# Keys and values of each token tile in a buffer of their own, in a ring of eight

## The chip, the cores and the metric

The kernel runs on one core of one Trainium2 chip. The metric is the device time of one execution in microseconds; the median over several executions counts. Before the change three executions took 2259.31, 2259.92 and 2261.94 us, with a median of 2259.92 us.

## What is computed

The reference is one transformer block over 32 sequences of 512 tokens with 256 features, all in float32. The first half is attention over a window of 128 tokens with 16 query heads and 4 key and value heads of width 64; the second half is a linear layer with eight gated low-rank corrections.

```python
x = x + attn(layernorm(x))      # q = x @ wq.T, k = x @ wk.T, v = x @ wv.T
                                # q, k = rmsnorm(q), rmsnorm(k), per head
                                # mask = (i >= j) & (i - j < 128)
                                # softmax(q @ k.T / 8, masked) @ v, then @ wo.T
x = x + ffn(layernorm(x))       # xt @ weight.T + 1/16 * sum over the experts of
                                # softmax(xt @ gate_w.T) * (xt @ U.T) @ V.T
```

## The kernel before

The 32 sequences are cut into 128 token tiles of 128 tokens, four to a sequence. The host lays the weights out, and the core keeps them in SBUF for the whole run. Because the window is as long as a tile, a token tile needs only its own keys and values and those of the tile before it in the same sequence.

The work is a software pipeline whose order is written out by hand. The function `slot(i)` lists, for one step, which part of which tile comes next, and the program calls it for i from 0 to 134. The order of that list is the order of the instructions in the queue of every engine: TensorE (PE), VectorE (DVE), ScalarE (ACT), GpSimd (POOL) and SyncE (SP). No scheduler moves anything. A tile is spread over eight slots: in slot i the projections of tile i are made, in slots i + 2 and i + 3 its scores and exponentials, in slot i + 4 the probabilities are transposed and moved by DMA, in slot i + 6 they are multiplied by the values, and in slot i + 7 the second half ends and the result is stored. Waits between engines are semaphore waits that the language puts in: one wherever an instruction touches a buffer, or a bank of PSUM, that another engine uses, unless an earlier wait in the same queue has already covered it.

Keys and values of a tile come out of one product, `kv_pe` (L289), into a PSUM bank named `kv_ps`, with 256 columns of keys and 256 of values. Four steps use that bank:

- `ksq` (L300), on ScalarE, squares the keys for their norm.
- `vdiff` (L471 and L474), on VectorE, forms `vd`, the difference between the tile's own values and those of the tile before it. It reads the own values from `kv_ps` and the old ones from the SBUF buffer `kv`. It does nothing for the first tile of a sequence, so it runs for 96 of the 128 tiles.
- `kv_copy` (L296), on ScalarE, scales keys and values and writes them to the SBUF buffer `kv`.

In `slot` these stand in the order `ksq(i)`, `vdiff(i)`, `kn(i - 1)`, `kv_copy(i)`, `qn(i - 1)`, `kT_copy(i - 2)`.

The SBUF buffer `kv` is read in three places: by `kn` (L337, GpSimd), which normalises the keys in slot i + 1; by `vdiff` of the next tile, also in slot i + 1; and by `y_pe` (L485, TensorE), where it is the stationary operand of the products with the probabilities. `y_pe` of a tile reads the values of that tile and of the one before, so the values of tile i are read for the last time in slot i + 7.

Before the change, one buffer holds keys and values of a whole sequence. It is taken when the first tile of the sequence is written, and there are three of them:

```python
if self.t == 0:
    self.s.kv = seq.tile([P, NT, 2 * KD], F32, tag="kv", name=f"kv_{self.b}", bufs=3)
nc.scalar.activation(self.s.kv[:, self.t, :], self.ps["kv"], AF.Copy, scale=self.ln1.rs)
```

Of the kernel before, what the change touches and what calls it, by code (L numbers as in the profile page):

```python
# [8 lines left out]
F32 = mybir.dt.float32  # L9
I32 = mybir.dt.int32  # L10
AF = mybir.ActivationFunctionType
# [3 lines left out]
P = 128  # L15
D = 256
HD = 64
# [13 lines left out]
def tile_window_attn_lora_ffn(  # L31
# [42 lines left out]
    nc = tc.nc  # L74
    B, T, _ = x.shape
    NT = T // P
# [4 lines left out]
    KD = KV * HD  # L81
# [14 lines left out]
    seq = ctx.enter_context(tc.tile_pool(name="seq", bufs=3))  # L96
# [16 lines left out]
    def bank(what, name):  # L113
# [19 lines left out]
        "other": 3,  # L133
        "tr": 2,
        "pT": 2,
    }

    def buf(what, shape, name):
        return work.tile(shape, F32, tag=what, name=f"{what}_{name}", bufs=BUFS[what])
# [109 lines left out]
    class Tile:  # L249
# [41 lines left out]
                )  # L291

        def kv_copy(self):
            if self.t == 0:
                self.s.kv = seq.tile([P, NT, 2 * KD], F32, tag="kv", name=f"kv_{self.b}", bufs=3)
            nc.scalar.activation(self.s.kv[:, self.t, :], self.ps["kv"], AF.Copy, scale=self.ln1.rs)  # L296

        def ksq(self):
            self.k_sq = buf("ksq", [P, KD], self.n)
# [35 lines left out]
        def kn(self):  # L335
            self.k_n = buf("kn", [P, KD], self.n)
            nc.gpsimd.tensor_tensor(  # L337
                self.k_n.rearrange("p (g d) -> p g d", d=HD),
                self.s.kv[:, self.t, :KD].rearrange("p (g d) -> p g d", d=HD),
                self.rs[:, NH:].unsqueeze(2).to_broadcast([P, KV, HD]),  # L340
                ALU.mult,
            )
# [121 lines left out]
        def vdiff(self):  # L464

            if self.t == 0:
                return
            self.vd = buf("vd", [P, KD], self.n)
            own, old = self.ps["kv"][:, KD:], self.s.kv[:, self.t - 1, KD:]
            lo, hi = slice(0, H), slice(H, P)  # L470
            nc.vector.scalar_tensor_tensor(  # L471
                self.vd[lo], own[lo], self.ln1.rs[lo], old[lo], ALU.mult, ALU.subtract
            )
            nc.vector.scalar_tensor_tensor(  # L474
                self.vd[hi], own[hi], self.minus_rs[hi], old[hi], ALU.mult, ALU.add
            )

        def y_pe(self):


            ps = [self.bank(f"y{e}") for e in range(2)]

            def product(gp, half, e, v, w, start, stop):
                v0 = (2 * gp + half) * HD
                nc.tensor.matmul(  # L485
                    ps[e][half * HD : (half + 1) * HD, gp * 4 * H : (gp + 1) * 4 * H],
                    v[:, v0 : v0 + HD],
                    w.rearrange("p h (c a q) -> p a h c q", c=2, a=2)[:, half],
                    start=start, stop=stop, skip_group_check=True,
                )  # L490

            for gp in range(GP):
                for e in range(2):
                    v = self.s.kv[:, max(self.t - 1 + e, 0), KD:]
                    for half in range(2):
                        product(gp, half, e, v, self.probs(gp, e), gp == 0, self.t == 0)
            if self.t > 0:
                for gp in range(GP):
                    for half, e in ((0, 0), (1, 1), (1, 0), (0, 1)):
                        rows = slice(e * H, (e + 1) * H)  # L500
                        product(gp, half, e, self.vd[rows], self.other[gp][rows], False, True)
# [92 lines left out]
    tiles = {}  # L594
# [132 lines left out]
```

## Time and profile before

| what | value |
|---|---|
| median of three executions | 2259.92 us |
| the profiled execution: its own time | 2258.15 us |
| the profiled execution: its span, first to last instruction | 2256.2 us |
| mean granted TensorE clock | 0.989 |
| busy: PE, POOL, DVE, ACT | 2145.9, 1807.1, 1734.7, 1508.3 us |
| `kv_copy` L296: 128 instructions, mean | 686 ns |
| `vd` L471 and L474: 96 instructions each, mean | 473 and 491 ns |
| `kn` L337: 128 instructions, mean | 612 ns |
| products `y_ps<-pT,kv` L485: 2048 instructions, busy | 250.1 us |

The span is the time between the first and the last instruction on the core; the execution's own time has 1.95 us more around it. A product in float32 appears in the trace as more than one matrix instruction, so the counts on TensorE are larger than those in the source. A wait in the trace names the engine that sat idle and the instruction whose end released it; idle time of an engine that is not on the chain that ended last costs nothing by itself.

### The profile page before, as it was taken

What the parts mean: (1) busy time and instruction counts of PE and PEld (TensorE: products, weight loads), DVE (VectorE), ACT (ScalarE), POOL (GpSimd) and SP (SyncE); (2) the same over time, 40 slices, a digit from 0 to 9 for tenths busy, and PEclk for the clock granted to TensorE, in tenths of its full rate; (3) what the DMA queues carried; (4) which work ended last, traced back from release to release, by engine and by line L of the source; (5) the groups of instructions that cost most, each with busy time, mean ns of one, the idle gap of its engine ahead of it and who ended that gap; (6) DMA issues with size and microseconds to landing.
All of it is one profiled execution on the core that took longest, in us unless ns stands there. A gap on an engine that the chain in (4) does not pass through costs nothing.

```text
span 2256.2 us, 43995 instructions
## 1 busy us (share of the span) xinstructions
PE 2145.9 (95%) x12688; PEld 1340.5 (59%) x12688; DVE 1734.7 (77%) x4300; ACT 1508.3 (67%) x5889; POOL 1807.1 (80%) x1771
## 2 busy tenths in 40 slices
PE   5799999999999999999999999999999999999997
PEld 2366566666566666566666566666566666566654
DVE  3577877777877777877777877777877777877773
ACT  2567667767767767767767767767767767767762
POOL 3598788888888888888888888888888888888873
PEclk8799999999999999999999999999999999999999
DMA  2344444544544454544544544544544544544542
GB/s 93 72 111 116 119 118 114 120 118 114 120 118 114 118 120 114 123 116 114 122 117 113 123 116 114 123 116 113 123 116 114 123 116 113 123 116 114 123 112 65
DMA packets 140127, 257.77 MB, mean 114 GB/s; under 512 B 37872, under 2 KB 73840, under 8 KB 139888
## 3 DMA queue, kind: packets, MB, share of 16 engines
q1 hardware_dynamic: 137472, 251.81, 46.5%
q10 hardware_dynamic: 2416, 3.16, 0.4%
q8 instruction: 103, 1.69, 0.3%
q14 instruction: 136, 1.11, 0.2%
HBM read 19.93 MB, written 16.78 MB: 16 GB/s over the span
## 4 chain that ended last, share of the span: by engine, by line
PE 66%; ACT 17%; DVE 9%; issue 4%; SPq 2%; DMA 1%; POOL 1%; ACTq 1%; DVEq 0%; POOLq 0%
PE y_ps L485 14%; PE s_ps L387 13%; PE q_ps L305 12%; ACT ex L414 12%; PE kv_ps L289 8%; PE f_ps L543 7%; PE o_ps L512 5%; PE f_ps L581 2%; ACT kT L369 2%; DVE nmax L403 2%; PE hT_ps L530 2%; DVE vd L474 2%; DVE vd L471 2%; SPq L244 2%; PE xT_ps L277 1%
## 5 line engine op out<-in xcount | busy, mean ns | idle before, releaser
L414 ACT ACTIVATE ex<-s_ps,nmax 128x128 f32<-128x128 f32 x2048 | 722.1, 381 | 13.2 <-DVE nmax L403 11.7
L426 POOL TENSOR_TENSOR ex<-ex,rden 128x1024 f32<-128x1024 f32 x256 | 479.9, 1896 | 130.9 <-DVE rden L422 125.8
L305 PE MATMUL q_ps<-wq_sb,xT 128*128 128x512 f32 x1024 | 489.0, 600 | 3.2 <-ACT qsq L318 3.2
L512 PE MATMUL o_ps<-wo_sb,yT 128*128 128x256 f32 x2048 | 463.5, 379 | 3.7 <-ACT yT L506 3.7
L214 POOL TENSOR_TENSOR rs<-rs,minus_half 128x20 f32<-128x20 f32 x128 | 457.5, 3574 | 10.7
L512 PEld LDWEIGHTS o_ps<-wo_sb,yT 128*128 128x128 f32 x2048 | 388.6, 190 | 110.2 <-issue 58.4
L414 ACT ACTIVATION_READ_ACCUMULATOR ex<-s_ps,nmax 128x1 f32 x2048 | 454.0, 222 | 0.0
L387 PEld LDWEIGHTS s_ps<-kT,pT 64*128 64x128 f32 x4000 | 276.5, 187 | 194.6 <-ACT ex L414 135.6
L387 PE MATMUL s_ps<-kT,pT 64*128 64x160 f32 (+4 forms) x4000 | 329.7, 300 | 45.9 <-ACT ex L414 45.9
L403 DVE TENSOR_REDUCE nmax<-s_ps 128x4 f32<-128x512 f32 x512 | 353.8, 691 | 17.6
L457 POOL TENSOR_SCALAR_AFFINE_SELECT other<-pT 64x512 f32<-64x512 f32 x384 | 299.9, 781 | 22.2 <-DMA pT<-tr 9.5
L305 PEld LDWEIGHTS q_ps<-wq_sb,xT 128*128 128x128 f32 x1024 | 187.2, 193 | 150.1 <-issue 129.4
L437 DVE STREAM_TRANSPOSE tr<-ex 128x256 f32<-128x256 f32 (+3 forms) x512 | 239.7, 487 | 29.1 <-DMA pT<-tr 25.0
L289 PE MATMUL kv_ps<-wkv_sb,xT 128*128 128x512 f32 x512 | 257.8, 626 | 1.0 <-ACT xT L283 1.0
L485 PE MATMUL y_ps<-pT,kv 128*64 128x256 f32 x2048 | 250.1, 386 | 0.5 <-ACT xT L283 0.5
L506 ACT COPY yT<-y_ps 128x512 f32<-128x512 f32 x256 | 138.6, 599 | 160.6 <-PE y_ps L485 160.6
L346 POOL TENSOR_TENSOR qn<-q,rs 128x1024 f32<-128x1024 f32 x128 | 243.4, 1901 | 0.0
L398 DVE COPY_PREDICATED s_ps<-over,s_ps 128x128 f32<-128x128 int32 x512 | 149.5, 292 | 98.9 <-PE s_ps L387 94.4
L300 ACT ACTIVATE ksq<-kv_ps,ln_rs_a 128x256 f32<-128x256 f32 x128 | 60.6, 473 | 243.3 <-PE kv_ps L289 232.3
L485 PEld LDWEIGHTS y_ps<-pT,kv 128*64 128x64 f32 x2048 | 136.1, 137 | 128.0 <-ACT q L313 50.8
L543 PE MATMUL f_ps<-wf_sb,hT 128*128 128x392 f32 x512 | 193.2, 500 | 18.0 <-ACT xT L283 12.1
L313 ACT ACTIVATE q<-q_ps,ln_rs_a 128x512 f32<-128x512 f32 x256 | 182.7, 714 | 27.9 <-PE q_ps L305 27.9
(83 smaller groups left out, 2716.3 us busy)
## 6 DMA issues: line engine op xcount, KB each, us to landing
pT<-tr SPq DMA_DIRECT2D x2000, 104.0 KB, 2.2
x<-in_x_dram SPq DMA_DIRECT2D x128, 128.0 KB, 2.3
out_dram<-res SPq DMA_DIRECT2D x128, 128.0 KB, 1.9
pT<-tr SPq DMA_DIRECT2D x48, 64.0 KB, 2.0
wq_sb<-in_wq_dram ACTq DMA_DIRECT2D x1, 1024.0 KB, 7.1
wo_sb<-in_wo_dram ACTq DMA_DIRECT2D x1, 1024.0 KB, 9.3
pT_-3_205<-tr_-3_199 SPq DMA_DIRECT2D x16, 40.0 KB, 1.9
pT_-2_274<-tr_-2_268 SPq DMA_DIRECT2D x16, 40.0 KB, 1.9
```

The costliest lines, as they stand in the source:

```text
L214: nc.gpsimd.tensor_tensor(o, o, minus_half[:, :n], ALU.pow)
L289: nc.tensor.matmul(ps, self.xT[:, c, :], wkv_sb[:, c, :], start=(c == 0), stop=(c == ND - 1))
L305: nc.tensor.matmul(ps, self.xT[:, c, :], wq_sb[:, c, gp * 512 : (gp + 1) * 512], start=(c == 0), stop=(c == ND - 1),)
L346: nc.gpsimd.tensor_tensor(self.q_n.rearrange("p (g d) -> p g d", d=HD), self.q.rearrange("p g (h d) -> p (g h) d", d=HD), self.rs[:, :NH]. ...
L387: nc.tensor.matmul(ps[:, half, gp, o0:n], qT[rows, gp * P : (gp + 1) * P], self.s.kT[rows, gp, k0 + o0 : k0 + n], start=True, stop=True,)
L403: nc.vector.tensor_reduce(self.nmax[j], ps[:, :, :, :P], AX.X, ALU.max, negate=True)
L414: nc.scalar.activation(self.ex[e][:, c, gp, half], ps[:, gp, half, :P], AF.Exp, bias=self.nmax[j][:, gp, half : half + 1], accum_out=self. ...
L426: nc.gpsimd.tensor_tensor(ex, ex, self.rden[e].rearrange("p c g a -> p (c g a)").unsqueeze(2).to_broadcast([P, 8, P]), ALU.mult,)
L457: nc.gpsimd.affine_select(out=self.other[gp][rows].rearrange("p h (c a q) -> p h c a q", c=2, a=2), in_=fr.rearrange("p h (c a q) -> p h c ...
L485: nc.tensor.matmul(ps[e][half * HD : (half + 1) * HD, gp * 4 * H : (gp + 1) * 4 * H], v[:, v0 : v0 + HD], w.rearrange("p h (c a q) -> p a ...
L512: nc.tensor.matmul(ps[:, :D], self.yT[:, c].rearrange("p e t -> p (e t)"), wo_sb[:, c, :], start=(c == 0), stop=(c == NCH - 1),)
L543: nc.tensor.matmul(ps[:, : UG + D], self.hT[:, c, :], wf_sb[:, c, :], start=(c == 0), stop=(c == ND - 1),)
```

## The change

Each tile gets a buffer of its own for its keys and values, 128 partitions by 512 floats, and eight of these buffers are used in turn. The first tile of a sequence no longer takes a larger buffer. The readers name the buffer of the tile they want in place of a slice of the sequence's buffer. In a partition the ring takes 8 x 2 KiB = 16 KiB, where three sequence buffers of 8 KiB took 24 KiB. No line of `slot` is changed.

```diff
@@ the table of buffer counts
         "pT": 2,
+        "kv": 8,
@@ kv_copy
-            if self.t == 0:
-                self.s.kv = seq.tile([P, NT, 2 * KD], F32, tag="kv", name=f"kv_{self.b}", bufs=3)
-            nc.scalar.activation(self.s.kv[:, self.t, :], self.ps["kv"], AF.Copy, scale=self.ln1.rs)
+            self.kv = buf("kv", [P, 2 * KD], self.n)
+            nc.scalar.activation(self.kv, self.ps["kv"], AF.Copy, scale=self.ln1.rs)
@@ kn
-                self.s.kv[:, self.t, :KD].rearrange("p (g d) -> p g d", d=HD),
+                self.kv[:, :KD].rearrange("p (g d) -> p g d", d=HD),
@@ vdiff
-            own, old = self.ps["kv"][:, KD:], self.s.kv[:, self.t - 1, KD:]
+            own, old = self.ps["kv"][:, KD:], tiles[self.i - 1].kv[:, KD:]
@@ y_pe
-                    v = self.s.kv[:, max(self.t - 1 + e, 0), KD:]
+                    v = tiles[self.i - 1 + e if self.t > 0 else self.i].kv[:, KD:]
```

## The prediction

> **What bounds the kernel now.** I read the page's first part, then the chain that ended last, then the waits, and then every row in which the buffer `kv` is written or read. The first part and the chain:
>
> ```profile
> span 2256.2 us, 43995 instructions
> ...
> PE 2145.9 (95%) x12688; PEld 1340.5 (59%) x12688; DVE 1734.7 (77%) x4300; ACT 1508.3 (67%) x5889; POOL 1807.1 (80%) x1771
> ...
> PE 66%; ACT 17%; DVE 9%; issue 4%; SPq 2%; DMA 1%; POOL 1%; ACTq 1%; DVEq 0%; POOLq 0%
> PE y_ps L485 14%; PE s_ps L387 13%; PE q_ps L305 12%; ACT ex L414 12%; PE kv_ps L289 8%; PE f_ps L543 7%; PE o_ps L512 5%; PE f_ps L581 2%; ACT kT L369 2%; DVE nmax L403 2%; PE hT_ps L530 2%; DVE vd L474 2%; DVE vd L471 2%; SPq L244 2%; PE xT_ps L277 1%
> ```
>
> TensorE is busy 95% of the span and carries 66% of the chain. The rest goes mostly over ScalarE (17%) and VectorE (9%). The two instructions of `vdiff` are themselves on the chain with 2% each: so what stands around `kv_copy` matters, and a change of its waits could be seen. The waits that concern this step, from the list of who waited for whom (total us, times, longest us):
>
> ```profile
> ACT ksq L300 <- PE kv_ps L289: 232.3, 125, 5.9
> ACT kv L296 <- DVE vd L474: 115.7, 96, 1.7
> PE s_ps L387 <- ACT ex L414: 61.0, 101, 3.8
> DVE vd L471 <- ACT ksq L300: 31.8, 65, 3.3
> ```
>
> ScalarE sits idle 115.7 us in all, 1.2 us in each of 96 tiles, in front of `kv_copy`, until `vdiff` is done. That is the only wait in front of any writer or reader of `kv` that is worth a name, and the only one that the change could seem to lift. In time order, over one and a half slots (start us, length us):
>
> ```profile
> 975.80 0.61 PE L485 MATMUL y_ps<-other,vd 64*64 64x256 f32 x8
> ...
> 979.71 0.47 ACT L300 ACTIVATE ksq<-kv_ps,ln_rs_a 128x256 f32<-128x256 f32 x1 [1.89 <-PE kv_ps L289]
> 980.22 0.48 DVE L471 SCALAR_TENSOR_TENSOR vd<-kv_ps,ln_rs_a,kv 64x256 f32<-64x256 f32 x1 [0.54 <-ACT ksq L300]
> 980.71 0.49 DVE L474 SCALAR_TENSOR_TENSOR vd<-kv_ps,minus_rs,kv 64x256 f32<-64x256 f32 x1
> 981.24 0.69 ACT L296 ACTIVATE kv<-kv_ps,ln_rs_a 128x512 f32<-128x512 f32 x1 [1.05 <-DVE vd L474]
> ...
> 997.35 0.69 ACT L296 ACTIVATE kv<-kv_ps,ln_rs_a 128x512 f32<-128x512 f32 x1 [1.05 <-DVE vd L474]
> ```
>
> `ksq`, the two halves of `vd` and `kv_copy` follow one another and never overlap. All four read the PSUM bank `kv_ps`. `vd` waits for `ksq`, with which it shares no SBUF buffer that `ksq` writes, so what orders those two can only be the bank. By the same reasoning `kv_copy` waits for `vd` because of the bank: it writes slice t of `kv`, and `vd` reads slice t - 1.
>
> **What the Trainium skill says.** "PSUM — Partial Sum Buffer", section "PSUM bank collisions raise a hardware error", states that two engines must not be on the same bank and quadrant at once, reads against reads included, and that software must guard it with semaphores. The trace agrees: 96 waits of `kv_copy` for the 96 tiles that have a `vd`, and none for the 32 first tiles. "SBUF — State Buffer", section "Who interferes with whom", states that only the port pair shared by VectorE and GpSimd causes contention; nothing in it depends on the address within a partition. The trace agrees as far as it can, since `kv` before lies at 12 places (three buffers of four slices) and its rows have hardly any spread (min/median/max ns):
>
> ```profile
> L485 PEld LDWEIGHTS y_ps<-pT,kv x2048: 132/137/232, 110.5 to 2239.8; 128*64 128x64 f32 x187
> L296 ACT ACTIVATE kv<-kv_ps,ln_rs_a x128: 679/687/692, 18.3 to 2165.9; 128x512 f32<-128x512 f32 x128
> L337 POOL TENSOR_TENSOR kn<-kv,rs x128: 612/612/615, 30.0 to 2180.4; 128x256 f32<-128x256 f32 x128
> L471 DVE SCALAR_TENSOR_TENSOR vd<-kv_ps,ln_rs_a,kv x96: 465/476/477, 26.1 to 2164.9; 64x256 f32<-64x256 f32 x96
> L474 DVE SCALAR_TENSOR_TENSOR vd<-kv_ps,minus_rs,kv x96: 490/491/494, 26.6 to 2165.4; 64x256 f32<-64x256 f32 x96
> ```
>
> "DMA: Bandwidth & Descriptors", section "How a descriptor splits into AXI transactions", states that a transfer's start is counted in steps of 256 bytes. That matters because buffers move (below); no run here shows a misaligned transfer.
>
> **The change part by part.**
>
> *Instructions.* The four edits name other addresses and add or remove nothing. In the two programs as built, every engine has the same instructions in the same order: cost 0.
>
> *The wait of `kv_copy` for `vd`.* It would go only if it came from the SBUF buffer. It comes from the bank, and in the changed program as built it is still there, for the same 96 copies: gain 0.
>
> *The wait for a free buffer.* Before, a buffer was reused 12 tiles later and asked for only at the first tile of a sequence; now every copy overwrites the buffer of the tile eight before. The last reader of tile i - 8 is `y_pe` of tile i - 7, in slot i - 1. The extract shows it: the last products of one slot start at 975.80 us and are over at 976.41, those that read `kv` even earlier, and the copy of the next slot starts at 997.35, 20.9 us later, more than one slot (981.24 to 997.35 is 16.1 us). The other readers, `kn` and `vd`, are done in slot i - 7. ScalarE has by then passed its own wait for the same products, in `y_copy` of slot i - 1, and waits on VectorE and GpSimd newer than the other readers. So nothing has to be waited for, and no waiting instruction has to be added; every semaphore wait in the two programs as built has the same semaphore and the same value. Cost 0. The cover is 20.9 us thick; it would shrink by one slot with seven buffers, and with six the reader would stand behind the writer.
>
> *Addresses.* This is all that is left. The ring frees 8 KiB in a partition, so all buffers laid out behind it move: `x`, `xT`, `kT` and `ksq` down by 24 KiB, `q`, `tr`, `pT`, `ex` and the rest by 8 KiB, `kv` itself up by 23 KiB. These are multiples of 256 bytes, so no transfer changes its alignment: the DMAs (`x` 2.3 us, `pT` 2.2 us from issue to landing) should stay as they are. For the instructions on `kv` I bound the effect from both sides by the spread of their own rows: `kv_copy` 13 ns x 128 = 1.7 us, `vd` (12 + 4) ns x 96 = 1.5 us, `kn` 3 ns x 128 = 0.4 us, together 3.6 us, were all of it on the path. The weight loads from `kv` take 137 ns beside products of 379, and are hidden even if they doubled. The DMA waits that are worth a name (VectorE 25.0, GpSimd 9.5, ScalarE 2.4 us for `pT`) are 36.9 us; an estimate of 5% either way for them gives 1.8 us. So between -5.4 and +5.4 us; I take 0, since no row shows a dependence on the place.
>
> *Sum.* Against the profiled execution: span 2256.2 + 0, with 1.95 us around it 2258.15 us. The median of the runs stands 1.77 us above that execution, so the forecast is 2259.9 us, no change.
>
> **The rivals.**
>
> *Faster: the wait for `vd` goes after all.* For it: 115.7 us of idle ScalarE, and `vd` on the chain. Then `kv_copy`, `kT_copy` and the exponentials behind it would run up to 1.2 us earlier in 96 tiles. What TensorE gains is bounded by what it loses to late exponentials, 61.0 us: 2259.9 - 61 = 2199 us; the outer bound is 2259.9 - 115.7 = 2144. Against it: the bank orders the two, and it still does. Chance 3%.
>
> *Slower: a new wait in front of each copy.* With eight buffers each copy, not each fourth, has to be sure of three readers on three engines. Were that one more waiting instruction on ScalarE's queue, it would stand in front of `kT_copy` and the exponentials that TensorE waits for. The chain in order of time shows what such an entry of ScalarE's sequencer costs (start us, length us):
>
> ```profile
> 1015.07 0.02 ACT kv L296
> 1015.09 0.04 issue
> 1015.13 0.04 ACTq L369
> 1015.17 0.04 issue
> ```
>
> That is 0.04 and 0.04 us, 0.08 x 128 = 10 us, so 2270 us, if the entry stands behind the wait for `vd`; ahead of it, the 1.2 us of idle would hide it. It decides from 35 ns per tile (4.5 us over 128). Against it: the waits as built are the same. Chance 3%.
>
> *The places matter.* Some row or transfer is longer or shorter at its new place by more than the spread above. Twice the bound is 11 us: 2249 or 2271. For it: nothing but that it is the only thing that differs. Chance 6%, half of it on each side.
>
> **How the numbers follow.** About 0.2%, 4.5 us, is what a measurement of this kernel can tell from no change; the three runs before alone span 2.63 us. No change has 88%, the lifted wait 3%, the new wait 3%, the places 3% and 3%: faster 0.06, same 0.88, slower 0.06. The range is that of the likeliest case: the bound of 5.4 us on both sides, 2254.5 to 2265.3; it leaves out the 12% of the other cases and is not widened for them.
>
> **What would show it.** In the changed kernel's profile, 43995 instructions; ScalarE's wait for `vd` again near 115.7 us in 96 places; no wait of `kv_copy` for TensorE or GpSimd; the rows of `kv` at 687, 612, 476 and 491 ns; the same products on the chain. A row of `kv` or a landing time that moved by over 5% would show that places count. A wait of `kv_copy` that is gone, or a new one, would make the prediction wrong.

## The result and the profile after

Over 14 executions each, the changed kernel takes a median of 2258.18 us and the kernel before 2258.95 us. The ratio is 0.9998, with a 95% interval from 0.9989 to 1.0006: no difference. The forecast was 2259.9 us and no change. One of the changed kernel's 14 executions, the profiled one, took 4627.46 us with TensorE's products about twice as long (those of `q_ps` 1216 ns on average, for 599); this came once in 27 executions of it, its cause is open, and the ratio leaves it out (the other 13 have a median of 2258.06 us). The profile shown here is that of a second measurement of the same changed kernel (the run `again` below: 2259.34 us, ratio 1.0002, 0.9994 to 1.001).

The first part of its page and its chain (PEld is TensorE's loading of weights, and L290 here is L289 of the kernel before, since the edit adds a line above it):

```profile
span 2257.4 us, 43995 instructions
...
PE 2145.7 (95%) x12688; PEld 1341.2 (59%) x12688; DVE 1735.5 (77%) x4300; ACT 1510.9 (67%) x5889; POOL 1809.4 (80%) x1771
...
PE 65%; ACT 16%; DVE 9%; issue 4%; SPq 2%; POOL 1%; DMA 1%; ACTq 1%; DVEq 0%; POOLq 0%
PE y_ps L485 14%; PE s_ps L387 13%; PE q_ps L305 12%; ACT ex L414 12%; PE kv_ps L290 7%; PE f_ps L543 7%; PE o_ps L512 5%; PE f_ps L581 2%; ACT kT L369 2%; DVE nmax L403 2%; PE hT_ps L530 2%; DVE vd L474 2%; SPq L245 2%; DVE vd L471 2%; ACT ksq L300 1%
```

The number of instructions is the same to the last one, TensorE's busy time differs by 0.2 us, and the chain is made of the same products with shares that differ by a point at most. The waits around `kv_copy` (who waited for whom: total us, times, longest us):

```profile
PEld s_ps L387 <- ACT ex L414: 154.5, 131, 4.6
...
ACT kv L296 <- DVE vd L474: 115.7, 96, 1.7
...
PE s_ps L387 <- ACT ex L414: 62.5, 101, 3.8
...
DVE vd L471 <- ACT ksq L300: 31.7, 65, 3.3
```

ScalarE is idle in front of `kv_copy` for 115.7 us in 96 places, as before the change, to the tenth of a microsecond. There is no wait of `kv_copy` for TensorE or GpSimd. The rows on `kv` (min/median/max ns):

```profile
L485 PEld LDWEIGHTS y_ps<-pT,kv x2048: 132/137/231, 109.1 to 2241.0; 128*64 128x64 f32 x187
L296 ACT ACTIVATE kv<-kv_ps,ln_rs_a x128: 680/687/690, 17.6 to 2165.1; 128x512 f32<-128x512 f32 x128
L337 POOL TENSOR_TENSOR kn<-kv,rs x128: 613/614/617, 29.3 to 2179.6; 128x256 f32<-128x256 f32 x128
L471 DVE SCALAR_TENSOR_TENSOR vd<-kv_ps,ln_rs_a,kv x96: 466/475/478, 25.4 to 2164.1; 64x256 f32<-64x256 f32 x96
L474 DVE SCALAR_TENSOR_TENSOR vd<-kv_ps,minus_rs,kv x96: 490/491/494, 25.9 to 2164.6; 64x256 f32<-64x256 f32 x96
```

The largest change of a median here is that of `kn`, from 612 to 614 ns. No other row moved further: of the groups of like instructions on ScalarE, VectorE and GpSimd with 90 members or more, none has a median that moved by more than 2 ns. So the result and each of its parts are as forecast. What remained to be tested is why: whether the wait comes from the bank and not from the buffer, whether the places and the depth of the ring really cost nothing, and whether the wait that stayed would have been worth anything.

### The profile page after: what moved, and what is told of

Its sections match the earlier page's. It is cut to its first block, busy times and chain, and to the rows that moved or that the text cites. A ratio compares the mean times of both kernels' runs of the same rounds, so it can differ in the third digit from the quotient of the medians.

```text
span 4625.5 us, 43995 instructions
## 1 busy us (share of the span) xinstructions
PE 4591.1 (99%) x12688; PEld 2205.9 (48%) x12688; DVE 1767.4 (38%) x4300; ACT 1534.1 (33%) x5889; POOL 1814.4 (39%) x1771
## 4 chain that ended last, share of the span: by engine, by line
PE 99%; ACT 1%; DVE 0%; issue 0%; DMA 0%; ACTq 0%; DVEq 0%
PE o_ps L512 22%; PE q_ps L305 22%; PE y_ps L485 15%; PE s_ps L387 14%; PE kv_ps L290 11%; PE f_ps L543 8%; PE f_ps L581 3%; PE hT_ps L530 1%; PE xT_ps L278 1%; PE uT_ps L574 1%; PE q_ps_mean L200 0%; ACT ex L414 0%; PE kv_ps_mean L200 0%; DMA wkv_sb<-in_wkv_dram 0%; PE f_ps_mean L200 0%
## 5 line engine op out<-in xcount | busy, mean ns | idle before, releaser
L305 PE MATMUL q_ps<-wq_sb,xT 128*128 128x512 f32 x1024 | 1075.0, 1216 | 2.7 <-ACT qsq L318 2.7
L512 PE MATMUL o_ps<-wo_sb,yT 128*128 128x256 f32 x2048 | 1029.6, 705 | 3.7 <-ACT yT L506 3.7
L512 PEld LDWEIGHTS o_ps<-wo_sb,yT 128*128 128x128 f32 x2048 | 644.6, 315 | 489.9 <-issue 471.7
L387 PEld LDWEIGHTS s_ps<-kT,pT 64*128 64x128 f32 x4000 | 521.8, 323 | 344.9 <-issue 310.8
L387 PE MATMUL s_ps<-kT,pT 64*128 64x160 f32 (+4 forms) x4000 | 632.8, 495 | 0.7 <-ACT ex L414 0.7
L290 PE MATMUL kv_ps<-wkv_sb,xT 128*128 128x512 f32 x512 | 533.8, 1218 | 1.0 <-ACT xT L284 1.0
L485 PE MATMUL y_ps<-pT,kv 128*64 128x256 f32 x2048 | 520.5, 709 | 0.5 <-ACT xT L284 0.5
L305 PEld LDWEIGHTS q_ps<-wq_sb,xT 128*128 128x128 f32 x1024 | 310.9, 305 | 436.8 <-issue 427.2
L543 PE MATMUL f_ps<-wf_sb,hT 128*128 128x392 f32 x512 | 411.6, 976 | 4.0 <-DVE res L588 4.0
L506 ACT COPY yT<-y_ps 128x512 f32<-128x512 f32 x256 | 140.6, 588 | 717.3 <-PE y_ps L485 717.3
L485 PEld LDWEIGHTS y_ps<-pT,kv 128*64 128x64 f32 x2048 | 191.3, 185 | 378.4 <-issue 334.7
L327 DVE TENSOR_REDUCE ss<-qsq 128x16 f32<-128x1024 f32 x128 | 156.2, 1220 | 421.8 <-ACT qsq L318 421.8
```

The lines of the kernel that those rows point to most:

```text
L290: nc.tensor.matmul(ps, self.xT[:, c, :], wkv_sb[:, c, :], start=(c == 0), stop=(c == ND - 1))
L305: nc.tensor.matmul(ps, self.xT[:, c, :], wq_sb[:, c, gp * 512 : (gp + 1) * 512], start=(c == 0), stop=(c == ND - 1),)
L387: nc.tensor.matmul(ps[:, half, gp, o0:n], qT[rows, gp * P : (gp + 1) * P], self.s.kT[rows, gp, k0 + o0 : k0 + n], start=True, stop=True,)
L485: nc.tensor.matmul(ps[e][half * HD : (half + 1) * HD, gp * 4 * H : (gp + 1) * 4 * H], v[:, v0 : v0 + HD], w.rearrange("p h (c a q) -> p a ...
L512: nc.tensor.matmul(ps[:, :D], self.yT[:, c].rearrange("p e t -> p (e t)"), wo_sb[:, c, :], start=(c == 0), stop=(c == NCH - 1),)
L543: nc.tensor.matmul(ps[:, : UG + D], self.hT[:, c, :], wf_sb[:, c, :], start=(c == 0), stop=(c == ND - 1),)
```

## The experiments

Each kernel was measured beside the kernel before on the same chip; that took 2259.33 us beside `ring7`, `aligned` and `copy_first_seq`, and 2259.24 us beside the others. Medians and ratios to it:

| run | edit | median us | ratio (95%) |
|---|---|---|---|
| `again` | the changed kernel | 2259.34 | 1.0002 (0.9994 to 1.001) |
| `ring12` | twelve buffers | 2258.95 | 1.0 (0.9992 to 1.0009) |
| `ring7` | seven buffers | 2258.9 | 0.9995 (0.9989 to 1.0002) |
| `aligned` | buffers on multiples of 256 bytes | 2259.25 | 0.9997 (0.999 to 1.0004) |
| `copy_first` | `kv_copy` ahead of `vdiff` | 2200.3 | 0.9742 (0.9728 to 0.9755) |
| `copy_first_seq` | the same, one buffer per sequence | 2199.49 | 0.9729 (0.9716 to 0.9742) |
| `vd_sbuf` | `copy_first`, and `vdiff` reads SBUF alone | 2237.66 | 0.9904 (0.9891 to 0.9918) |

### The change once more, and the depth of the ring

`again` is the changed kernel, unaltered.

> The changed kernel once more, unaltered[...]. Renaming only (my theory): within 0.2% of the kernel before (4.5 us), 43995 instructions, kv_copy idle for vd near 115.7 us in 96 places, rows on kv at 687, 612, 476 and 491 ns. Places matter: another ratio clear of 1, or a row on kv or a landing time of x or pT moved by over 5%. The wait goes: ScalarE has no idle time for vd in front of kv_copy, and the time is near 2199 us.

All of it came as the renaming has it; the lines stand above. With separate buffers `kv_copy` writes nothing that `vd` reads, and yet it waits for `vd` for 115.7 us in 96 places. A wait that outlives the buffer that it might have come from comes from the other thing that the two share, the PSUM bank `kv_ps`. What stays open is whether the buffer of a whole sequence would have ordered the two by itself: no run takes the bank away from the kernel before.

`ring12` and `ring7` change one number:

```diff
-        "kv": 8,
+        "kv": 12,        # ring7: 7
```

> A ring of twelve buffers in place of eight: 24 KiB in a partition, as before the change, so that q, tr, pT, ex and all behind them lie again at the addresses that they have before the change, while kv is still one buffer per tile and is reused twelve tiles later. Renaming only: within 0.2% of before and of the ring of eight. Places matter: this one agrees with the kernel before and the ring of eight does not. A short ring costs something: this one is faster than the ring of eight, up to 10 us (0.08 us in 128 copies).

> A ring of seven, the smallest that can run: the copy of slot i overwrites what the products of the same slot have read. Its waits and instructions as built are those of the ring of eight, since ScalarE's y_copy of the same slot has already waited for those products. My theory: within 0.2% of before. If a shorter ring costs: slower, up to 10 us.

Both are within 0.2% of the kernel before, and of the ring of eight. `ring12` puts `q`, `tr`, `pT` and `ex` back to where they lie before the change, and that makes no difference either. In time order, `ring7` shows how thin its cover is (start us, length us):

```profile
989.49 1.95 PE L485 MATMUL y_ps<-pT,kv 128*64 128x256 f32 x16
991.07 1.11 ACT L506 COPY yT<-y_ps 128x512 f32<-128x512 f32 x2
996.25 0.69 ACT L296 ACTIVATE kv<-kv_ps,ln_rs_a 128x512 f32<-128x512 f32 x1 [1.05 <-DVE vd L474]
```

With seven buffers, the copy at 996.25 us overwrites what the products of its own slot have read by 991.44 us: 4.8 us are left of a cover of more than a slot. Over all tiles the cover is 4.7 to 6.2 us with seven buffers, and 22.0 to 22.9 us with eight. Between the products and the copy stand the two instructions of ScalarE's `y_copy` (L506). The second of them reads what the last of these products wrote, so by then ScalarE has waited for them anyway, and the copy waits for `vd` alone. Six buffers were not tried.

### The places

`aligned` moves all buffers that are used in turn by 160 bytes. In the kernel before and in the changed one these start 96 bytes past a multiple of 256; here they start on one.

```diff
+    pad = const.tile([P, 40], F32, name="pad")
+    nc.vector.memset(pad, 0.0)
```

> The changed kernel with 160 bytes of padding ahead of all moving buffers (and one fill of the padding on VectorE before the loop, below 0.3 us), so that tr, pT, x and kv start on multiples of 256 bytes, where they start 96 bytes off in the kernel before and in the changed one. Places don't matter: within 0.2% of before. Places matter through the alignment of transfers, as the Trainium skill's page DMA: Bandwidth & Descriptors states: landing of pT below 2.2 us and less DMA share; the time could fall by up to the waits for pT, 36.9 us, but more likely by 0 to 5 us since transfers are hidden.

The time is the same. The queue of the loop's transfers (packets, MB, share of 16 engines), first in `again` and then in `aligned`:

```profile
q1 hardware_dynamic: 137472, 251.81, 46.5%
...
q1 hardware_dynamic: 137472, 251.81, 45.5%
```

The transfer that matters (KB each, median us to landing) and the wait for it, in `aligned`:

```profile
pT<-tr SPq DMA_DIRECT2D x2000, 104.0 KB, 2.2
...
DVE tr L439 <- DMA pT<-tr: 26.0, 115, 0.6
```

The share of the queue is 45.5% where the changed kernel has 46.5% (46.5% before, too): the transfers take about 2% less of the DMA engines. The packets of 3328 bytes, those of `pT`, take 220.9 ns on average for 225.0. The landing of `pT` stays at 2.2 us and VectorE's waits for it at 26.0 us (`again` has 2.2 and 26.0 us as well). The Trainium skill, "DMA: Bandwidth & Descriptors", section "How a descriptor splits into AXI transactions", says that a start off the 256-byte grid costs beats, which are steps of 32 bytes; the share and the packets agree in direction, and the time does not show it.

### What the wait for vd is worth

`copy_first` moves one line of `slot` in the changed kernel; `copy_first_seq` does the same in the kernel before.

```diff
         at(i).ksq()
+        at(i).kv_copy()
         at(i).vdiff()
         at(i - 1).kn()
-        at(i).kv_copy()
```

> The changed kernel with kv_copy written straight behind ksq, ahead of vdiff, so that VectorE's vd waits for ScalarE's kv_copy and not the other way round; both still take turns on the PSUM bank. It measures what the wait of 115.7 us is worth. If my bound in the rival is right and the exponentials behind it are what TensorE waits for: up to 61 us faster, 2199 us, and the waits of PE for ex fall from 61 us. If TensorE only waits elsewhere instead: within 0.2% of before, ScalarE idle somewhere else, and PE idle about as before. vd starts later by one kv_copy, 0.69 us, less what the copy gains.

> The kernel before, with its buffer per sequence, and kv_copy written ahead of vdiff as in the run copy_first. If the order on the bank is all that counts and the buffers nothing: the time of copy_first, 2200 us within 0.2%. If copy_first needed a buffer per tile: slower than that, up to 2259 us.

In the queue of each engine the order of the instructions stays as it was: on ScalarE `kv_copy` still follows `ksq`, on VectorE `vdiff` still comes ahead of `ksum`. What the edit turns round is who waits for whom. Both kernels are 2.6 to 2.7% faster than the kernel before, by 59 us (2259.24 - 2200.3) and 60 us (2259.33 - 2199.49), and the buffers make no difference that can be told: 0.9742 and 0.9729 have overlapping intervals. In `copy_first` the copy follows `ksq` at once, and the exponentials with it:

```profile
984.07 0.47 ACT L300 ACTIVATE ksq<-kv_ps,ln_rs_a 128x256 f32<-128x256 f32 x1 [1.64 <-PE kv_ps L290]
984.44 0.68 ACT L296 ACTIVATE kv<-kv_ps,ln_rs_a 128x512 f32<-128x512 f32 x1
985.01 0.51 ACT L369 ACTIVATE kT<-pT,key_w 128x256 f32<-128x256 f32 x1
985.15 0.48 DVE L471 SCALAR_TENSOR_TENSOR vd<-kv_ps,ln_rs_a,kv 64x256 f32<-64x256 f32 x1
985.41 0.36 ACT L414 ACTIVATE ex<-s_ps,nmax 128x128 f32<-128x128 f32 x1
985.65 0.49 DVE L474 SCALAR_TENSOR_TENSOR vd<-kv_ps,minus_rs,kv 64x256 f32<-64x256 f32 x1
```

From the start of `ksq` to the first exponential it is 985.41 - 984.07 = 1.34 us. In `again` the same stretch reads:

```profile
978.60 0.47 ACT L300 ACTIVATE ksq<-kv_ps,ln_rs_a 128x256 f32<-128x256 f32 x1 [1.88 <-PE kv_ps L290]
979.11 0.48 DVE L471 SCALAR_TENSOR_TENSOR vd<-kv_ps,ln_rs_a,kv 64x256 f32<-64x256 f32 x1 [0.54 <-ACT ksq L300]
979.60 0.49 DVE L474 SCALAR_TENSOR_TENSOR vd<-kv_ps,minus_rs,kv 64x256 f32<-64x256 f32 x1
980.13 0.69 ACT L296 ACTIVATE kv<-kv_ps,ln_rs_a 128x512 f32<-128x512 f32 x1 [1.05 <-DVE vd L474]
980.71 0.50 ACT L369 ACTIVATE kT<-pT,key_w 128x256 f32<-128x256 f32 x1
981.11 0.36 ACT L414 ACTIVATE ex<-s_ps,nmax 128x128 f32<-128x128 f32 x1
```

That is 981.11 - 978.60 = 2.51 us, 1.17 us more. For this `vd` starts 1.08 us after the start of `ksq` in place of 0.51 us. The waits of `copy_first` and its chain:

```profile
DVE vd L471 <- ACT kv L296: 68.0, 64, 3.9
...
PEld s_ps L387 <- ACT ex L414: 43.2, 46, 3.5
...
PE s_ps L387 <- ACT ex L414: 21.8, 11, 3.0
```

```profile
span 2197.4 us, 44091 instructions
...
PE 2127.4 (97%) x12688; PEld 1331.9 (61%) x12688; DVE 1728.5 (79%) x4300; ACT 1509.4 (69%) x5889; POOL 1807.2 (82%) x1771
...
PE 93%; SPq 3%; ACT 2%; DMA 1%; POOL 1%; DVE 1%; issue 0%; ACTq 0%; DVEq 0%; POOLq 0%
```

The wait did not vanish, it changed sides: VectorE now waits 68.0 us for a copy into a buffer of its own, which `vd` does not read. That is the bank once more. But VectorE is not on the chain: ScalarE and VectorE fall from 16% and 9% of it to 2% and 1%, and TensorE goes from 65% to 93%. TensorE's matrix products wait 21.8 us for the exponentials where they waited 62.5 us, 40.7 us less. The other 18.3 us of the fall of the span from 2257.4 to 2197.4 us are TensorE's busy time, the time in which at least one product runs, which goes from 2145.7 to 2127.4 us with the same 12688 instructions; together that is 59.0 of 60.0 us.

What the second share is can be read where the granted clock is 1.00 in both profiles, from the first product of `kv_ps` for the ninth tile to that for the 121st (window, its length, TensorE's busy time, granted clock, DMA), first in `again` and then in `copy_first`:

```profile
146.93:2043.21 1896.28, 1848.58 (x11091) 1.00 0.49 117
...
140.03:1989.28 1849.25, 1837.47 (x11090) 1.00 0.50 120
```

Here TensorE needs 47.0 us less; 35.9 us of it are idle time and 11.1 us busy time. The products themselves are not shorter: added up one by one, those of this stretch take 4242.9 us in `again` and 4245.2 us in `copy_first`. So they overlap more, which fits a queue that stops less often. The ends of overlapping products are modelled in the trace, so the split into idle and overlap is a property of the records, the 47.0 us are not. The other 13.0 us of the 60.0 lie in the first tiles and the last, where the granted clock differs between the two profiles (0.989 and 0.992 over the whole span); they were not taken apart.

The edit also adds 96 instructions that only wait. Of these, 5 are in VectorE's queue, and 91 in TensorE's, in front of the transpose `uT_ps` (L574): it is the next to write this bank, and now has two engines to wait for. The span still falls by 60 us.

### Without the bank

`vd_sbuf` starts from `copy_first` and takes `vdiff` off the bank:

```diff
-            own, old = self.ps["kv"][:, KD:], tiles[self.i - 1].kv[:, KD:]
+            own, old = self.kv[:, KD:], tiles[self.i - 1].kv[:, KD:]
...
-            nc.vector.scalar_tensor_tensor(
-                self.vd[lo], own[lo], self.ln1.rs[lo], old[lo], ALU.mult, ALU.subtract
-            )
-            nc.vector.scalar_tensor_tensor(
-                self.vd[hi], own[hi], self.minus_rs[hi], old[hi], ALU.mult, ALU.add
-            )
+            nc.vector.tensor_tensor(self.vd[lo], own[lo], old[lo], ALU.subtract)
+            nc.vector.tensor_tensor(self.vd[hi], old[hi], own[hi], ALU.subtract)
```

> As copy_first, and vdiff reads the tile's own values from the SBUF buffer kv, already scaled, and not from the PSUM bank: two subtractions with both inputs in SBUF. No pair of instructions of ScalarE and VectorE is left on the bank kv_ps. If the bank is what orders kv_copy behind vd: ScalarE has no idle time for vd in front of kv_copy at all. Time: as copy_first, 2199 to 2264 us. If a buffer per tile were what counts, kv_copy would still wait for vd.

ScalarE has no idle time in front of `kv_copy`, but as the copy stands first here, it could have had none in any case: on the question of bank or buffer this run is no test, and the expectation was badly put. Its time is a surprise. It is 1% faster than the kernel before, but 37 us slower than `copy_first` (2237.66 - 2200.3). Its rows of `vd` (min/median/max ns) and the stretch in time order:

```profile
L471 DVE TENSOR_TENSOR vd<-kv,kv x96: 416/1556/2099, 27.1 to 2144.3; 64x256 f32<-64x256 f32 x96
L472 DVE TENSOR_TENSOR vd<-kv,kv x96: 422/883/2033, 27.6 to 2145.8; 64x256 f32<-64x256 f32 x96
```

```profile
1001.77 1.90 POOL L346 TENSOR_TENSOR qn<-q,rs 128x1024 f32<-128x1024 f32 x1
1002.25 0.51 ACT L369 ACTIVATE kT<-pT,key_w 128x256 f32<-128x256 f32 x1
1002.39 1.56 DVE L471 TENSOR_TENSOR vd<-kv,kv 64x256 f32<-64x256 f32 x1
1003.62 1.89 POOL L457 TENSOR_SCALAR_AFFINE_SELECT other<-pT 64x512 f32<-64x512 f32 x2
1003.96 0.88 DVE L472 TENSOR_TENSOR vd<-kv,kv 64x256 f32<-64x256 f32 x1
```

At best a half of `vd` takes 416 ns, at the median 1556 and 883 ns. The first starts while GpSimd's `qn` runs and ends 0.28 us after it. The Trainium skill, "SBUF — State Buffer", section "Who interferes with whom", says that a VectorE instruction with two inputs in SBUF contends with a GpSimd instruction that reads SBUF, and that the later one waits. The trace agrees, on all 192 halves. Of these, 37 meet none of GpSimd's `kn`, `qn` and `other`, and they take 416 to 424 ns; 153 start while `qn` or `other` runs, and end 261 to 283 ns after it; the last two start beside `kn`. With one input in PSUM and one in SBUF, `vd` never took over 494 ns beside the same `qn`: neither before the change, where it runs from 980.22 us (above, in the prediction) and `qn` from

```profile
979.70 1.90 POOL L346 TENSOR_TENSOR qn<-q,rs 128x1024 f32<-128x1024 f32 x1
```

nor in `copy_first`, where 92 of the 96 first halves run beside `qn` and take 467 to 478 ns. So the long rows come with the overlap and the second input in SBUF together. No run moves `qn` out of the way, and the instruction differs too: it is a subtraction alone, without the scaling.

How this reaches TensorE is in the chain of `vd_sbuf` and in TensorE's waits there:

```profile
PE 78%; DVE 12%; ACT 4%; SPq 2%; issue 2%; DMA 1%; POOL 1%; ACTq 0%; POOLq 0%; DVEq 0%
...
PE f_ps L539 <- DVE res L584: 39.5, 36, 1.3
```

In `copy_first` the same product had these waits:

```profile
PE f_ps L543 <- ACT xT L284: 12.4, 30, 0.4
...
PE f_ps L543 <- DVE res L588: 4.5, 6, 1.2
```

VectorE's busy time grows from 1728.5 us in `copy_first` to 1824.4 us, and its share of the chain from 1% to 12%. Its last instruction for a tile, `res`, reads the bank into which the next `f_ps` goes, and comes late: TensorE is idle in front of `f_ps` for 39.5 us, where it was for 12.4 + 4.5 = 16.9 us. Its wait for the exponentials, which `copy_first` had shortened, grows less, from 21.8 to 26.3 us.

## Why the prediction was right

- **Instructions, cost 0.** Shown: 43995 instructions in both profiles, and busy times within 0.2% of each other.
- **The wait for `vd`, gain 0.** Shown twice: it stays at 115.7 us in 96 places with a buffer per tile, and with the order turned round VectorE waits for a copy into a buffer that it doesn't read. The bank orders them. One sentence on the way there was a misreading: the wait of `kv_copy` is not the only one of note in front of a writer or reader of `kv`. The prediction's own list has `vd` waiting 31.8 us for `ksq`, and TensorE's loads of `kv` (L485) wait 50.8 us in 91 places for ScalarE's copy of `q`. Both stayed, at 31.7 and 50.8 us in `again`, so nothing hung on it.
- **The wait for a free buffer, cost 0.** Shown for eight, for twelve and, with a cover of 4.7 us and more, for seven. The statement on six stays an argument.
- **Places, between -5.4 and +5.4 us, taken as 0.** Shown by `ring12` and `aligned` within what can be measured. The bound was narrower than its reasoning allows: it counted the rows on `kv` and the waits for `pT`, and not the other buffers that moved, such as `x`, `q` and `ex`. The rows show that these did not count either, with no median on ScalarE, VectorE or GpSimd off by more than 2 ns. The reason given for the transfers was half of one: the moves by multiples of 256 bytes kept an alignment that was off the grid by 96 bytes from the start, so every transfer of the loop was misaligned already. Putting it right moves the DMA share by a point and the time by nothing that can be told.
- **The rival that the wait goes: 2199 us.** It did not happen, and its price can now be put beside a measurement, since `copy_first` takes the wait off ScalarE: 2200.3 us. The size was right, the term only in part: of the 61 us of late exponentials that bounded it, 40.7 us went, and 18.3 us came as shorter busy time, from products that overlap more and from the ends of the run, which the prediction did not count. TensorE gained in a way that the bound does not cover, and the agreement to 1 us is partly luck.
- **The rival of a new waiting instruction in front of each copy: 2270 us.** No run has one; the price of 0.08 us for each was not tested.

The version that beats both kernels is `copy_first`, or `copy_first_seq` with the buffers of before, at 2199 to 2200 us.

## What to carry to other kernels

Before a buffer is split to lift a wait, look for what else the two instructions share. Here the wait between two readers that have only a PSUM bank in common stayed at 115.5 to 115.7 us, however the SBUF buffers were cut; but which of the two goes first was free, and letting ScalarE, with TensorE's work queued behind it, go ahead of VectorE, with slack, was worth 2.6%. Where a bank is avoided by reading SBUF instead, look at what GpSimd runs at that time.

## What was not expected

Two subtractions on VectorE that read SBUF alone took 1556 and 883 ns at the median beside GpSimd's work, up to 2099 ns, and 416 ns at best; the forms with one input in PSUM took 476 and 491 ns with hardly any spread. Starting the buffers used in turn on multiples of 256 bytes lowered the share of the DMA queue from 46.5% to 45.5% and left the landing time of `pT` at 2.2 us.
